# The first product of a graph convolution in seven block products, spread over four places of an LSTM pipeline

## The chip, the cores and the metric

The kernel runs on one core of a Trainium2 chip. The metric is the device time of one execution in microseconds (us). The core's engines run their own instruction queues side by side: TensorE (PE; its weight loads are listed as PEld), VectorE (DVE), ScalarE (ACT), GpSimd (POOL) and SyncE (SP), which here only starts transfers. All numbers are float32.

## The reference

Four layers work on x of 128 batches x 64 tokens x 256 channels. Each has the form x = x + f(relu(layernorm(x))). What matters here is layer 1, in which adj is the 64 x 64 adjacency matrix:

```python
h = relu(einsum('ts,bsh->bth', adj, x @ Wg0 + bg0))      # first graph convolution
h = relu(einsum('ts,bsh->bth', adj, h @ Wg1 + bg1))      # second graph convolution
for p in range(1, 5):                                    # four LSTMs, over windows of p tokens
    wins = h[:, :nw * p].reshape(B * nw, p, H)           # nw = T // p
    last = lstm_last(Wih[p-1], Whh[p-1], bih[p-1], bhh[p-1], wins)
    h = h.at[:, idx].set(last)                           # idx = p - 1, 2p - 1, ...
```

Each LSTM reads what the ones before it have written, so the four run one after another. Layer 0 is a network of two products with batch normalization, layers 2 and 3 are attention.

## The kernel before

The 8192 rows are cut into 16 chunks of 512 (index c), and the LSTM stage takes two chunks at a time: superchunk sc holds chunks 2sc and 2sc + 1, and runs the LSTMs for p = 1, 2, 3, 4 on them. The state lies with channels on the partitions, in two blocks of 128 (index k). A product of 256 x 256 weights with the state is made from seven products of 128 x 128 weight blocks, with sums and differences of blocks as operands: the function `differences` makes the four differences of the input blocks, and the sums of the weights are made once. In the LSTM steps the products of one gate add up in the PSUM banks x, y and z; between two products into a bank, ACT or DVE reads the partial sum.

While superchunk sc is in the LSTMs, the chunks of the next superchunk go through the two graph convolutions. `convolutions(c)` is a Python generator; what lies between two of its `yield`s is one unit. Its units in order: batch normalization (`scaled`), transposes, loads, the residual add (`add_squares`, L298), layer norm in four units, the product with adj (`aggregate`, L228), the copy from PSUM to SBUF (L1025), the product v with Wg0 (`product_v`, L934), its lower bound by a constant in place of bias and relu (`bounded`, L940), the product u with Wg1 (`product_u`, L948), its bias (`biased`, L954), and the second product with adj. In `product_u` the blocks of v are the weights that PE loads, and Wg1 is streamed.

The generator `lstms` yields too, and each of its yields has a number, its place. An ordinary yield goes on to the next whole number, a yield marked "a" to a half. The LSTM p=1 ends at place 3; p=2 has the places 4, 4.5, 5, 5.5, 6, 7; p=3 has 8 to 13; p=4 has 14, 14.5, 15 and so on to 21. Place 7 is after the last instruction of p=2, and place 13 after that of p=3. Lists say at which place each unit of a chunk is issued, the even chunk's list first:

```python
CONV = (3, 4, 5, 5.5, 7, 8, 9, 10, 10), (5, 5, 6, 9.5, 11, 11.5, 13, 14, 15, 15.5, 17, 18, 20)
BEGUN = (11, 11.5, 12, 14.5, 17, 17, 20, 21), (17.5, 19, 19.5, 21)
```

BEGUN holds the first units of the chunks after next, CONV the rest, FIRST stands for CONV in superchunk 0. The whole stage is under a manual schedule: each engine runs its instructions in the order in which the program issues them. Waits between engines are put in by the framework, from what an instruction reads and writes. At one place, the units of CONV come first, then those of the residual, of the next layer's work (`ahead`, lists AHEAD and LATE) and of BEGUN.

Before the change the even chunk has v at place 5, its bound at 5.5 and u at 7; the odd chunk has v at 13, its bound at 14 and u at 15. The DVE and ACT lines of the LSTM that are named further on: L1137 and L1192 copy a partial sum, L1140 and L1195 add one, L1101 is a gate's activation, L1158, L1165, L1265 and L1266 update the cell, L1159, L1166 and L1267 are its tanh, L1110, L1112 and L1116 write the new state, L327 to L330 are the four lines of `differences`. On GpSimd, L1252 multiplies two gates, and L99 and L100 belong to the layer norm.

PSUM has eight banks in this stage, of which the tag "ps" has two: they hold in turn the results of the products with adj, v and u. The SBUF tag "g" has three buffers, for transposed tiles of the residual and of the next layer. Chunks 0 and 1 go through `first_convolutions` in a start stage, where Wg0, Wg1 and LSTM weights are also loaded.

## Time and profile before

| | us |
|---|---|
| median of 3 runs (1841.59 to 1841.98) | 1841.59 |
| the profiled execution | 1841.82 |
| span of its records | 1839.9 |
| PE busy | 1813.3 (99%) |
| PE weight loads busy | 1531.8 (83%) |
| DVE busy | 1353.8 (74%) |
| ACT busy | 1061.4 (58%) |
| GpSimd busy | 656.8 (36%) |

The LSTM stage takes some 1210 us of the span, about 152 for each of the eight superchunks. The clock granted to PE was 0.999 of full speed. The profile lists two records for each matmul of 256 or 512 columns; [...]the time of a block is read from the chain or from the starts of its first and next instruction. In a line of the timeline the columns are: start in us, length in us, engine, line of the kernel, operation, what it writes and reads, its shape, how many instructions were merged, and, in brackets, the idle time of the engine before it and what ended that.

### The profile page before, as it was taken

The numbers are of one execution on the slowest core, as the hardware profiler recorded it, in microseconds if no ns is written. First come the engines' busy times: TensorE is split into PE (matmuls) and PEld (weight loads), VectorE is DVE, ScalarE is ACT, GpSimd is POOL, SyncE is SP. The second block draws the span as 40 slices with busy tenths as digits, with TensorE's granted clock in tenths as the row PEclk, the third lists the DMA queues.
The fourth block names the chain that finished last, engine by engine and source line by source line (L and its number), as shares of the span: only waits on it lengthen the run. The fifth ranks groups of instructions, "written<-read, shape, count | busy, mean of one in ns | idle before, by whom it ended". The sixth has DMA issues, their size and how long they took to land.

```text
span 1839.9 us, 41662 instructions
## 1 busy us (share of the span) xinstructions
PE 1813.3 (99%) x15847; PEld 1531.8 (83%) x15847; DVE 1353.8 (74%) x3475; ACT 1061.4 (58%) x2538; POOL 656.8 (36%) x916
## 2 busy tenths in 40 slices
PE   8999999999999999999999999999999999999998
PEld 6876866997897899699699789879968887898886
DVE  5768857577667777777777777776676677888897
ACT  5766636557457466655655746566565654455553
POOL 5865823223223321422321332232232215444542
PEclk9999999999999999999999999999999999999999
DMA  3213651233443342253443434225154146544534
GB/s 117 70 58 139 222 218 53 81 115 127 134 143 127 112 153 78 98 146 116 149 149 127 149 115 162 101 93 150 48 172 149 64 110 195 162 139 139 162 108 147
DMA packets 113415, 234.54 MB, mean 127 GB/s; under 512 B 11712, under 2 KB 77120, under 8 KB 113216
## 3 DMA queue, kind: packets, MB, share of 16 engines
q1 hardware_dynamic: 112320, 230.02, 38.5%
q8 instruction: 125, 2.05, 0.5%
q0 software_dynamic: 320, 1.05, 0.2%
q10 hardware_dynamic: 576, 0.82, 0.1%
q14 instruction: 74, 0.61, 0.1%
HBM read 164.21 MB, written 67.63 MB: 126 GB/s over the span
## 4 chain that ended last, share of the span: by engine, by line
PE 89%; DVE 5%; ACT 2%; POOL 2%; issue 1%; DMA 0%; SPq 0%; DVEq 0%; ACTq 0%; POOLq 0%
PE x L1186 23%; PE z L1186 11%; PE y L1186 6%; PE y L1133 4%; PE x L1368 4%; PE y L1368 3%; PE u L948 3%; PE v L934 3%; PE x L1133 3%; PE X L1938 3%; PE X L436 2%; PE X L512 2%; PE v L2062 2%; PE z L1133 2%; PE Y L1938 1%; PE X L1773 1%
## 5 line engine op out<-in xcount | busy, mean ns | idle before, releaser
L1101 ACT ACTIVATE l_gates<-l_gates,bias 128x256 f32<-128x256 f32 (+4 forms) x528 | 238.2, 498 | 210.9 <-DVE l_gates L1195 109.7
L1186 PE MATMUL x<-xd,wset 128*128 128x128 f32 (+2 forms) x1152 | 255.0, 303 | 0.8 <-ACT l_gates L1192 0.8
L1186 PE MATMUL x<-l_hd,wset 128*128 128x128 f32 (+2 forms) x1152 | 254.6, 303 | 0.0
L1252 POOL TENSOR_TENSOR l_gates<-l_gates 128x512 f32<-128x512 f32 (+2 forms) x48 | 75.3, 1570 | 368.0 <-ACT l_gates L1101 368.0
L1195 DVE TENSOR_TENSOR l_gates<-l_gates,x 128x128 f32<-128x128 f32 (+2 forms) x384 | 121.2, 321 | 97.8 <-PE x L1186 95.1
L1186 PEld LDWEIGHTS x<-xd,wset 128*128 128x128 f32 x1152 | 187.7, 191 | 6.4 <-issue 1.4
L1186 PEld LDWEIGHTS x<-l_hd,wset 128*128 128x128 f32 x1152 | 187.8, 191 | 5.0
L1195 DVE TENSOR_TENSOR l_gates<-l_gates,z 128x128 f32<-128x128 f32 (+2 forms) x384 | 102.3, 318 | 105.7 <-PE z L1186 103.7
L1186 PE MATMUL z<-l_hs,wset 128*128 128x128 f32 (+2 forms) x768 | 147.1, 304 | 0.7 <-DVE l_hs L1110 0.7
L1186 PE MATMUL z<-hT,wset 128*128 128x128 f32 (+2 forms) x768 | 146.2, 303 | 0.0
L1192 ACT COPY l_gates<-y 128x128 f32<-128x128 f32 (+2 forms) x192 | 53.2, 290 | 137.7 <-PE y L1186 131.5
L1186 PEld LDWEIGHTS z<-l_hs,wset 128*128 128x128 f32 x768 | 116.8, 191 | 5.8 <-DVE l_hs L1110 2.5
L1186 PEld LDWEIGHTS z<-hT,wset 128*128 128x128 f32 x768 | 117.1, 191 | 3.3
L1101 ACT ACTIVATE l_gates<-x,bias 128x128 f32<-128x128 f32 (+2 forms) x216 | 84.8, 393 | 28.6 <-PE x L1186 25.9
L327 POOL TENSOR_TENSOR xd<-hT 128x128 f32<-128x128 f32 (+2 forms) x72 | 43.2, 600 | 127.5 <-DVE hT L1112 113.8
L1186 PE MATMUL x<-hT,wset 128*128 128x128 f32 (+2 forms) x384 | 85.8, 305 | 0.0
L1186 PE MATMUL x<-l_hs,wset 128*128 128x128 f32 (+2 forms) x384 | 84.9, 303 | 0.0
L1186 PE MATMUL y<-l_hd,wset 128*128 128x128 f32 (+2 forms) x384 | 83.2, 309 | 0.0
L1267 ACT ACTIVATE l_gates<-l_cell 128x256 f32<-128x256 f32 (+2 forms) x144 | 55.3, 384 | 45.8 <-DVE l_cell L1266 45.3
L1186 PE MATMUL y<-xd,wset 128*128 128x128 f32 (+2 forms) x384 | 81.6, 304 | 0.0
L328 POOL TENSOR_TENSOR xd<-hT 128x128 f32<-128x128 f32 (+3 forms) x80 | 51.5, 644 | 67.0 <-DVE hT L1116 29.5
L1110 DVE TENSOR_TENSOR l_hs<-l_gates 128x256 f32<-128x256 f32 (+4 forms) x120 | 51.4, 428 | 29.6 <-ACT l_gates L1159 13.8
(408 smaller groups left out, 4696.8 us busy)
## 6 DMA issues: line engine op xcount, KB each, us to landing
wset<-wfar SPq DMA_DIRECT2D x96, 896.0 KB, 8.4
hT<-far_h SPq DMA_DIRECT2D x124, 128.0 KB, 4.7
far_h<-hm SPq DMA_DIRECT2D x16, 512.0 KB, 3.0
far_n<-xs SPq DMA_DIRECT2D x16, 512.0 KB, 3.4
xs<-far_n SPq DMA_DIRECT2D x64, 128.0 KB, 2.8
far_x<-xs SPq DMA_DIRECT2D x16, 512.0 KB, 3.9
x<-far_x SPq DMA_DIRECT2D x64, 128.0 KB, 3.9
xt<-in_x_dram SPq DMA_DIRECT2D x15, 512.0 KB, 3.9
```

The costliest lines, as they stand in the source:

```text
L328: lambda: ((third or engine).tensor_tensor(t3, b22, b12, OP.subtract), engine.tensor_tensor(t2, b22, t1, OP.subtract)),
L934: nc.tensor.matmul(banks[m], wg0_sb[:, k, m * P : (m + 1) * P], agg[:, k, :], start=(k == 0), stop=(k == KD - 1))
L948: nc.tensor.matmul(banks[j // 2][:, j % 2, :], v[:, k, j * P : (j + 1) * P], wg1_sb[:, k, :], start=(k == 0), stop=(k == KD - 1))
L1101: nc.scalar.activation(gate(q, c, part), src, AF.Tanh if q == 2 else AF.Sigmoid, bias=bs[:, q * KD + c : q * KD + c + 1])
L1133: nc.tensor.matmul(folded(self.psum(kind)), wsets[p, self.q][:, BLOCKS[kind][0], :], ox[0][kind], start=kind in (1, 5), stop=True, skip_gr ...
L1186: nc.tensor.matmul(folded(self.psum(kind)), wsets[p, self.q][:, BLOCKS[kind][i], :], (ox[self.s] if part == "x" else oh)[kind], start=firs ...
L1192: nc.scalar.copy(gate(self.q, kind // 5, halves[kind // 5]), self.psum(kind))
L1195: nc.vector.tensor_add(gate(self.q, *dst), gate(self.q, *a), self.psum(kind))
L1252: nc.gpsimd.tensor_mul(gates[:, 0, :, :n], gates[:, 0, :, :n], gates[:, 2, :, :n])
L1267: nc.scalar.activation(gate(2, c, part), cells[:, c, part], AF.Tanh)
L1368: nc.tensor.matmul(folded(ps(g, kind)), single_block(KINDS1[kind])[:, g, :], right[kind], start=kind in (2, 5, 1), stop=True, skip_group_c ...
L1938: nc.tensor.matmul(st[c, tag][:, i * CH // 2 : (i + 1) * CH // 2].rearrange("p (a n) -> p a n", n=P), w, operand3(c, kind), start=first an ...
```

## The change

Chunks 2 to 15 no longer make v by four products of 512 columns (two blocks of Wg0 for each half of the output). The new class `SevenV` makes it by seven products of 256 columns. After the copy from PSUM, GpSimd makes the four differences of the input's blocks in a tile of tag "g". The seven products go into two PSUM banks, the first called xx and zz by its halves, of the second only yy is used, in four units: products 2, 1 and 5 with ACT's copies of xx and yy into the input's own place; products 6 and 3 with one copy and one add; product 7 with two adds and two bounds; product 4 with the last bound, which reads PSUM. The last block of v comes to lie in the place of another one, so that `product_u` reads two blocks swapped; it takes the second half of the tokens first.

The lists get two entries more for each chunk: the even chunk has the four units at 5, 5.5, 6 and 7 and u at 7, the odd chunk at 13, 14, 14.5 and 15 and u at 15. Sums of the blocks of Wg0 are made once on GpSimd in the start stage. The bias bg1 is loaded into the tile c2 itself, and its own tile goes.

```diff
@@ start stage
-        bg1_sb = const.tile([P, D], F32, name="bg1_sb")
-        nc.sync.dma_start(bg1_sb, bg1.partition_broadcast(P))
+    nc.sync.dma_start(c2, bg1.partition_broadcast(P))
...
-                nc.vector.tensor_add(c2, c2_ps[:, :D], bg1_sb)
+                nc.vector.tensor_add(c2, c2, c2_ps[:, :D])
...
                 load_sets(6)
+                sums_of_wg0()
@@ product_u
-    def product_u(c, v):
+    def product_u(c, v, swapped=False):
+
         banks = [bank(f"u1_{c}_{t}").rearrange("p (j d) -> p j d", d=D) for t in range(NJ // 2)]
-        for j in range(NJ):
+        for j in (2, 3, 0, 1) if swapped else range(NJ):
             for k in range(KD):
-                nc.tensor.matmul(banks[j // 2][:, j % 2, :], v[:, k, j * P : (j + 1) * P],
+                at = (j + 2) % NJ if swapped and k else j
+                nc.tensor.matmul(banks[j // 2][:, j % 2, :], v[:, k, at * P : (at + 1) * P],
                                  wg1_sb[:, k, :], start=(k == 0), stop=(k == KD - 1))
         return banks
+
+    wg0_sums = w1.tile([P, 4, P], F32, name="wg0_sums")
+
+    def sums_of_wg0():
+        def a(k, m):
+            return wg0_sb[:, k, m * P : (m + 1) * P]
+
+        for d, u, v, op in ((0, a(0, 1), a(1, 1), OP.add), (1, wg0_sums[:, 0], a(0, 0), OP.subtract),
+                            (2, a(0, 0), a(0, 1), OP.subtract), (3, a(1, 0), wg0_sums[:, 1], OP.subtract)):
+            nc.gpsimd.tensor_tensor(wg0_sums[:, d], u, v, op)
+
+    class SevenV:
+
+        def __init__(self, c, y):
+            self.c, self.y = c, y
+            b = {(k, j): y[:, k, halves2[j]] for k in range(KD) for j in range(2)}
+            t = l1r.tile([P, 4, CH // 2], F32, tag="g", name=f"tv_{c}", bufs=3)
+            t = [t[:, i] for i in range(4)]
+            for f in differences(nc.gpsimd, t, b[0, 0], b[0, 1], b[1, 0], b[1, 1]):
+                f()
+            self.at = {1: b[0, 0], 2: b[1, 0], 3: b[1, 1], 4: t[3], 5: t[0], 6: t[1], 7: t[2]}
+            self.to = {(0, 0): b[0, 0], (0, 1): b[0, 1], (1, 0): b[1, 1], (1, 1): b[1, 0]}
+
+        def product(self, kind, ps, first=False):
+            if kind in (1, 2, 4):
+                m, k = {1: (0, 0), 2: (0, 1), 4: (1, 1)}[kind]
+                w = wg0_sb[:, k, m * P : (m + 1) * P]
+            else:
+                w = wg0_sums[:, {5: 0, 6: 1, 7: 2, 3: 3}[kind], :]
+            nc.tensor.matmul(ps, w, self.at[kind], start=first, stop=True, skip_group_check=True)
+
+        def add(self, part, ps):
+            nc.vector.tensor_add(self.to[part], self.to[part], ps)
+
+        def bound(self, m, dst, src):
+            dst, src = [a.rearrange("p (a n) -> p a n", n=P) for a in (dst, src)]
+            nc.vector.tensor_tensor(dst, src, nc1[:, m, None, :].to_broadcast([P, dst.shape[1], P]), OP.max)
+
+        def places(self):
+            xz, w = bank(f"vx_{self.c}"), bank(f"vy_{self.c}")
+            xx, zz, yy = xz[:, : CH // 2], xz[:, CH // 2 :], w[:, : CH // 2]
+            self.product(2, zz, True)
+            self.product(1, xx)
+            nc.scalar.copy(self.to[0, 0], xx)
+            self.product(5, yy, True)
+            nc.scalar.copy(self.to[1, 1], yy)
+            yield
+            self.product(6, xx)
+            nc.scalar.copy(self.to[0, 1], xx)
+            self.add((0, 0), zz)
+            self.product(3, yy)
+            yield
+            self.add((0, 1), yy)
+            self.product(7, xx)
+            self.add((1, 1), xx)
+            self.bound(0, self.y[:, 0], self.y[:, 0])
+            self.bound(1, self.to[1, 1], self.to[1, 1])
+            yield
+            self.product(4, xx)
+            self.bound(1, self.to[1, 0], xx)
+            yield
@@ convolutions, after the copy from PSUM
-        yield
-        banks = product_v(c, y)
-        yield
-        bounded(y, banks)
-        yield
-        banks = product_u(c, y)
+        v = SevenV(c, y)
+        yield
+        yield from v.places()
+        banks = product_u(c, y, swapped=True)
@@ the lists of places
-    CONV = (3, 4, 5, 5.5, 7, 8, 9, 10, 10), (5, 5, 6, 9.5, 11, 11.5, 13, 14, 15, 15.5, 17, 18, 20)
+    CONV = ((3, 4, 5, 5.5, 6, 7, 7, 8, 9, 10, 10),
+            (5, 5, 6, 9.5, 11, 11.5, 13, 14, 14.5, 15, 15, 15.5, 17, 18, 20))
-    FIRST = (0.5, 0.5, 1, 3, 3, 4, 4, 5, 5.5, 7, 8, 9, 10, 10), (2, 3, 4, 5, 5, 5.5, 6, 9.5, 11, 11.5, 13, 14, 15, 15.5, 17, 18, 20)
+    FIRST = ((0.5, 0.5, 1, 3, 3, 4, 4, 5, 5.5, 6, 7, 7, 8, 9, 10, 10),
+             (2, 3, 4, 5, 5, 5.5, 6, 9.5, 11, 11.5, 13, 14, 14.5, 15, 15, 15.5, 17, 18, 20))
```

## The prediction, made before the changed kernel was run

> **What bounds the kernel now.** I read the busy shares first, then the busy time by stage, then single instructions around the convolutions. The page's first part and the stretch of the third superchunk (us; busy time of PE, weight loads, DVE, ACT, POOL; clock; DMA share):
> ```profile
> PE 1813.3 (99%) x15847; PEld 1531.8 (83%) x15847; DVE 1353.8 (74%) x3475; ACT 1061.4 (58%) x2538; POOL 656.8 (36%) x916
> ...
> 580.00:732.00 152.00, 151.97 (x1145) 130.59 (x1144) 112.19 (x310) 91.16 (x238) 44.54 (x64) 1.00 0.37 122
> ```
> In the LSTM stage TensorE is idle 0.03 us of 152. So every column taken from it is gained, every wait put into it is lost, and nothing later makes up for a wait. The chain that ended last prices v and u:
> ```profile
> 609.90 3.43 PE v L934 x8
> 635.78 3.45 PE u L948 x16
> 680.76 3.43 PE v L934 x8
> 690.29 3.46 PE u L948 x16
> ```
> v is 4 products of 512 columns in 3.43 us, u 8 products of 256 columns in 3.45, so one 256-column product costs 0.431. Each block stands where the LSTM has a latency to hide. The timeline around u of convolution 6 (place 7, first line group) and 7 (place 15):
> ```profile
> 639.71 0.99 DVE L1116 TENSOR_TENSOR hT<-l_gates 128x256 f32<-128x256 f32 x2
> 640.62 1.28 DVE L954 TENSOR_TENSOR cv<-u,c 128x512 f32<-128x512 f32 x2
> ...
> 690.13 3.62 PE L948 MATMUL u<-wg_sb,cv 128*128 128x256 f32 x16
> 691.34 0.29 DVE L327 TENSOR_TENSOR l_hd<-l_hs 128x128 f32<-128x128 f32 x1
> 691.61 1.29 DVE L298 TENSOR_TENSOR xs<-xs,cv 128x512 f32<-128x512 f32 x2
> 692.82 0.42 DVE L1165 TENSOR_TENSOR l_cell<-l_gates 128x256 f32<-128x256 f32 x1
> 694.71 0.29 DVE L330 TENSOR_TENSOR l_hd<-l_hs,l_hd 128x128 f32<-128x128 f32 x1
> ```
> DVE still works on the LSTM's state while PE runs u: at place 7 until 640.70 (u ran 635.62 to 639.07), at place 15 until 695.00 (u ran 690.13 to 693.58). Today u needs nothing from that stretch, as v was bounded at 623.21 and 684.37.

> [...] The trace agrees (L1158 0.69, L1140 0.42), so the new SBUF-to-SBUF bounds get these prices. [...] the trace has GpSimd 256-column differences at 734 and at 929 ns (L330, L329)[...].

> **The change, part by part** (14 convolutions, one even and one odd in each superchunk 0 to 6).

> Removed and put in on PE: 3.43 us against 7 x 0.431 = 3.02, a gain of 0.41 each, 5.8 us in all, if nothing waits.

> GpSimd: four differences of some 0.74 = 3.0 us. Even: they follow the p=2 operands (end 605.39), so the third product of place 5 finds them; nothing follows until 613.84. Odd: after the copies at 673.77 they push the gate product L1252 from 675.18 to some 676.8, done at 678.4; its reader L1266 starts at 680.75. Both hidden; without that cover p=3's cell would be late by the excess. The scratch tile shares three "g" buffers, but at most two others are live when it comes: I take no wait.

> ACT: three copies of 0.37 each.

> Even convolution, numbers of the third superchunk. Place 5: v's block shrinks to three products, 1.29 us, so PE arrives 2.14 early. y<-l_hd must wait for L327 (ends 611.61), 0.2. z<-l_hs would come at 614.6 but needs the second L1110, which ends at 615.71, as four norm statistics stand ahead of its L1165 on DVE: 1.1. PE is 0.8 early; in superchunks 0 and 1, with no such statistics, 1.9 early. Place 5.5 adds two products (0.86), place 6 one (0.43): 0.4 late (0.7 early). At place 6 DVE now has two adds and two bounds, 0.42 + 0.42 + 0.69 + 0.42 = 1.95, ahead of the L1195 at 629.78. That add must read bank x before PE's next product into it: DVE is done at 632.1, PE is there at 631.7, so 0.4 is lost. PE and the chain behind it are **0.83 late** (first two: 0.23 early). Place 7: product 4, then its bound on DVE, then u. The bound is **queued behind L1116**. PE does product 4 and five products of u (2.6 us) and then stops, since the sixth takes as weights what that bound writes. L1116 ends 4.73 us after u's old start (5.08 in superchunk 2); then the bound 0.42, a restart of 0.29 (in the start stage L940 ended at 268.08, u began at 268.37), and the three products left, 1.29. Against u's old 3.45: 4.73 + 0.83 + 0.42 + 0.29 + 1.29 - 3.45 = 4.11 late (4.46 in superchunk 2; 3.05 in 0 and 1). Everything of p=3 is behind u on PE. Sum: 4 x 4.11 + 4.46 + 2 x 3.05 = 27.0.

> Odd convolution. Place 13: PE is again 2.14 early, and loses it: the first products of p=4 wait for L1112 (682.31), and product 6 waits for the copy of xx, which ACT reaches only after L1267 (684.09). With place 14's two products PE is level at 685.4 (before: 685.36). Place 14.5: the 1.95 us of DVE now stand ahead of L298 and L1165, which followed each other without a gap, so L1165, the second L1110 and L330 come 1.95 later. Place 15: the last bound is queued behind L330. L330 ended 4.87 after u's start: 4.87 + 1.95 + 0.42 + 0.29 + 1.29 - 3.45 = 5.37 late. In superchunk 6 there is no L298 and L1165 waited for ACT (1300.85, now 1302.2): 4.29 + 1.35 + 2.00 - 3.45 = 4.19. Sum: 6 x 5.37 + 4.19 = 36.4.

> Start stage: the four weight sums (some 0.5 each, as L1745) wait for wg_sb, issued at 240.17 with 2.9 to land; they end near 245.2, ahead of GpSimd's next work at 247.36, so nothing. bg1 now lands in c2: the same transfer, but one that may wait for c2's space with the loads of x behind it on SP (231.56, needed at 245.38). No row shows that; a c2 wait of up to 10 us is hidden, earlier space could gain a little. I take 0, with -1 to +4.

> Sum: 27.0 + 36.4 = 63.4. The profiled execution took 1841.82 with a span of 1839.9; it lies 0.23 above the median of 1841.59. So **1905.0**.

> **The rivals.**
> *Waits are covered, faster.* If the last bound were done when PE reaches the sixth product of u, only the gain of 5.8 would stay: 1836. That decides at 2.6 us after u's place: DVE must be through by then. For it: PE has early products to do. Against: DVE is busy with the LSTM until 4.73 and 4.87 after it. 4%.
> *The bound doesn't hold u up, but the rest stands.* If DVE took it ahead of the state's work, place 5 and 6 would cost some 1.3 in five even convolutions (0 in two), and the odd ones some 2.8, as product 4 needs the add that DVE reaches at 692.4: 26, so 1868. Against: L954 and L298 stand on DVE exactly where their places put them. 8%.
> *u waits as a whole.* If a wait went by tile or bank, the five early products would wait too: 2.16 x 14 = 30 more, 1935. Against: a product took l_hd at 310.07 while L328, issued ahead of it for another part of l_hd, began only at 310.93; so waits go by part. Banks: the first half of u can take the bank freed at place 6. 10%.
> *It doesn't do what it says.* The code gives 7 products of 256 columns for 4 of 512; the records will show it. No chance given.

> **How the numbers follow.** The forecast has 78%: 1892 to 1918, by +-0.5 us in each of the 14 sums and the start's bounds. 1866 to 1922 takes in the second rival and leaves out the first and third, with tails some 18%. A difference of 0.2% (3.7 us) is about what a measurement of this kernel can tell from no change. Faster: the first rival and a little, 0.05; within it 0.02; slower 0.93.

> **What would show it.** PE idle for some 10 us (the lateness and the 0.41 gained, twice) in each of superchunks 0 to 6, each of these 161 to 162 us long in place of 152, and superchunk 7 as before. The largest waits of PE are weight loads of u, put down to the last bound, 14 of them, of 2 to 3 us; next the odd convolutions' product 4, some 1.9, put down to the adds of place 14.5; small ones at z<-l_hs after L1110. Work grows without binding: DVE by 3 x 0.42 + 0.69 + 2 x 0.42 - 1.36 = 1.43 for each convolution, 20 us in all, ACT by 14 x 1.1 = 15, GpSimd by 14 x 3.0 + 2 = 44. The step at u is wrong if its eight products run without a gap, and the step at place 14.5 if L1165 isn't later there; the forecast is wrong if PE's idle time in these superchunks stays under 3 us each.

## The result, and the profile after

The changed kernel takes 1922.29 us (median of 4 runs, 1921.84 to 1922.54), the kernel before 1841.72 beside it: a ratio of 1.0436 (95% interval 1.0424 to 1.0448), 80.6 us slower. The forecast was 1905.0, so 63.4 slower; the direction held, and the stops of PE came where they were forecast; the size fell 17.3 us short, and the time lies 0.29 us beyond the upper end of the range.

First the page's busy times and its chain that ended last (before, PE had 89% of that chain and DVE 5%), then the stretch of the third superchunk by stage, with the columns as shown before:

```profile
PE 1840.4 (96%) x15931; PEld 1558.4 (81%) x15931; DVE 1371.5 (71%) x3531; ACT 1071.4 (56%) x2580; POOL 696.3 (36%) x976
...
PE 80%; DVE 11%; ACT 4%; POOL 2%; issue 2%; DMA 1%; DVEq 0%; SPq 0%; ACTq 0%; POOLq 0%
```
```profile
605.49:769.47 163.98, 156.22 (x1158) 135.03 (x1157) 114.47 (x317) 93.05 (x245) 49.94 (x72) 0.98 0.34 113
```

Two things stand in that line. PE now idles for 7.8 us of the superchunk where it idled for 0.03. And it is busy for longer, 156.2 us in place of 152.0, although seven products of 256 columns are less work than four of 512, while its clock has a mean of 0.98 in place of 1.00. The superchunks 0 to 6 became longer by 13.5, 12.2, 12.0, 11.6, 10.8, 12.4 and 8.0, in all 80.5; the start and superchunk 7 are as before.

What PE waited for most in the superchunks 0 to 6 (us in total, times, longest):

```profile
PE u L949 <- DVE cv L988: 32.2, 14, 2.8
PE vx L981 <- DVE cv L984: 11.3, 7, 1.6
PE z L1246 <- DVE l_hs L1170: 4.0, 5, 0.8
```

L988 is the bound in `SevenV`, L984 its add, L981 its product, L949 the product of u. The other lines have moved: L1110, L1112 and L1116 are now L1170, L1172 and L1176, L1165 is L1225, L1186 is L1246, L1133 is L1193, L954 is L1016. Each of the 14 u stops, for the bound, as forecast. The timeline at place 7 of the third superchunk, lines of PE and DVE:

```profile
662.31 1.89 PE L949 MATMUL u<-wg_sb,cv 128*128 128x256 f32 x8
...
665.62 0.99 DVE L1176 TENSOR_TENSOR hT<-l_gates 128x256 f32<-128x256 f32 x2
666.53 0.42 DVE L988 TENSOR_TENSOR cv<-vx,nc 128x256 f32<-128x256 f32 x1
667.00 3.78 PE L949 MATMUL u<-wg_sb,cv 128*128 128x256 f32 x8 [2.80 <-DVE cv L988]
670.58 1.33 PE L1193 MATMUL y<-hT,wset 128*128 128x168 f32 x4
```

The bound starts as L1176 ends, and u goes on as the bound ends. But u has done only four products by then (8 records), not five, and its second half takes 3.58 us to the next instruction, where four products take 1.72 at full clock (4 x 0.431). The profile by stages of a few us shows why (the eighth column, after POOL's busy time, is the clock that was granted):

```profile
667.00:670.50 3.50, 3.50 (x8) 2.86 (x9) 0.00 (x0) 0.00 (x0) 3.34 (x8) 0.50 1.02 349
670.50:674.00 3.50, 3.50 (x17) 3.42 (x16) 1.29 (x2) 1.76 (x6) 1.94 (x4) 0.63 0.50 90
674.00:680.00 6.00, 6.00 (x76) 5.47 (x78) 3.93 (x13) 1.98 (x6) 0.00 (x0) 1.00 0.00 1
```

From 666.24 to 673.07 PE has half the clock, with u's second half and the first products of p=3 in it. This happens after 9 of the 14 stops; the trace shows the halved clock for 34.1 us of these superchunks, ten times 3.41, and PE is busy in 33.0 of them. Half of that, 16.5 us, is my estimate of what the halved clock costs.

The same place in the odd convolution, where the clock stayed whole (1.00 in each stretch from 722 to 740), PE first and then DVE:

```profile
724.86 0.70 PE L981 MATMUL vx<-tv,wg_sb 128*128 128x256 f32 x2 [1.62 <-DVE cv L984]
725.47 1.99 PE L949 MATMUL u<-wg_sb,cv 128*128 128x256 f32 x8
729.44 1.99 PE L949 MATMUL u<-wg_sb,cv 128*128 128x256 f32 x8 [1.98 <-DVE cv L988]
```
```profile
724.06 0.41 DVE L984 TENSOR_TENSOR cv<-cv,vy 128x256 f32<-128x256 f32 x1
724.39 0.41 DVE L984 TENSOR_TENSOR cv<-cv,vx 128x256 f32<-128x256 f32 x1
724.73 1.02 DVE L988 TENSOR_TENSOR cv<-cv,nc 128x512 f32<-128x512 f32 x2
725.66 1.29 DVE L298 TENSOR_TENSOR xs<-xs,cv 128x512 f32<-128x512 f32 x2
726.87 0.42 DVE L1225 TENSOR_TENSOR l_cell<-l_gates 128x256 f32<-128x256 f32 x1
...
728.76 0.29 DVE L330 TENSOR_TENSOR l_hd<-l_hs,l_hd 128x128 f32<-128x128 f32 x1
728.97 0.42 DVE L988 TENSOR_TENSOR cv<-vx,nc 128x256 f32<-128x256 f32 x1
```

Two adds and two bounds stand ahead of L298 and L1225, and the last bound stands behind L330. Both are where the prediction put them.

### The profile page after: what moved, and what is told of

The parts are those of the page before. It is cut to its first block, busy times and chain, and to the rows that moved or that the text cites. A ratio compares the mean times of both kernels' runs of the same rounds, so it can differ in the third digit from the quotient of the medians.

```text
span 1920.0 us, 41959 instructions
## 1 busy us (share of the span) xinstructions
PE 1840.4 (96%) x15931; PEld 1558.4 (81%) x15931; DVE 1371.5 (71%) x3531; ACT 1071.4 (56%) x2580; POOL 696.3 (36%) x976
## 4 chain that ended last, share of the span: by engine, by line
PE 80%; DVE 11%; ACT 4%; POOL 2%; issue 2%; DMA 1%; DVEq 0%; SPq 0%; ACTq 0%; POOLq 0%
PE x L1246 20%; PE z L1246 10%; PE y L1246 5%; PE x L1428 4%; PE y L1193 3%; PE y L1428 3%; PE u L949 3%; PE X L2001 2%; PE X L436 2%; PE x L1193 2%; PE X L512 2%; PE v L2125 2%; PE z L1193 1%; PE Y L2001 1%; DVE l_gates L1200 1%
## 5 line engine op out<-in xcount | busy, mean ns | idle before, releaser
L1246 PE MATMUL x<-xd,wset 128*128 128x128 f32 (+2 forms) x1152 | 255.4, 303 | 2.2 <-DVE l_gates L1255 1.4
L1246 PE MATMUL x<-l_hd,wset 128*128 128x128 f32 (+2 forms) x1152 | 254.5, 303 | 0.0
L1246 PEld LDWEIGHTS x<-xd,wset 128*128 128x128 f32 x1152 | 187.1, 191 | 9.1 <-DVE l_gates L1255 2.7
L1246 PEld LDWEIGHTS x<-l_hd,wset 128*128 128x128 f32 x1152 | 187.8, 191 | 5.0
L1246 PE MATMUL z<-l_hs,wset 128*128 128x128 f32 (+2 forms) x768 | 147.6, 305 | 4.7 <-DVE l_hs L1170 4.7
L1246 PE MATMUL z<-hT,wset 128*128 128x128 f32 (+2 forms) x768 | 146.2, 303 | 0.0
L1252 ACT COPY l_gates<-y 128x128 f32<-128x128 f32 (+2 forms) x192 | 53.2, 290 | 164.6 <-PE y L1246 162.3
L1246 PEld LDWEIGHTS z<-l_hs,wset 128*128 128x128 f32 x768 | 116.3, 191 | 11.6 <-DVE l_hs L1170 8.5
L1246 PEld LDWEIGHTS z<-hT,wset 128*128 128x128 f32 x768 | 117.6, 191 | 3.7
L949 PE MATMUL u<-wg_sb,cv 128*128 128x256 f32 x224 | 68.2, 458 | 32.2 <-DVE cv L988 32.2
L327 POOL TENSOR_TENSOR xd<-hT 128x128 f32<-128x128 f32 (+2 forms) x72 | 42.2, 587 | 124.8 <-DVE hT L1172 111.0
L949 PEld LDWEIGHTS u<-wg_sb,cv 128*128 128x128 f32 x224 | 48.3, 223 | 47.6 <-DVE cv L988 40.0
L1246 PE MATMUL x<-hT,wset 128*128 128x128 f32 (+2 forms) x384 | 85.8, 305 | 0.0
L1246 PE MATMUL y<-l_hd,wset 128*128 128x128 f32 (+2 forms) x384 | 84.8, 313 | 0.3
L1246 PE MATMUL x<-l_hs,wset 128*128 128x128 f32 (+2 forms) x384 | 84.8, 303 | 0.0
L1246 PE MATMUL y<-xd,wset 128*128 128x128 f32 (+2 forms) x384 | 83.0, 309 | 0.0
```

The lines of the kernel that those rows point to most:

```text
L327: return [lambda: engine.tensor_tensor(t1, b12, b11, OP.subtract), lambda: ((third or engine).tensor_tensor(t3, b22, b12, OP.subtract), en ...
L949: nc.tensor.matmul(banks[j // 2][:, j % 2, :], v[:, k, at * P : (at + 1) * P], wg1_sb[:, k, :], start=(k == 0), stop=(k == KD - 1))
L1246: nc.tensor.matmul(folded(self.psum(kind)), wsets[p, self.q][:, BLOCKS[kind][i], :], (ox[self.s] if part == "x" else oh)[kind], start=firs ...
L1252: nc.scalar.copy(gate(self.q, kind // 5, halves[kind // 5]), self.psum(kind))
```

## The experiments

My theory after the result: the stops at u cost what the prediction says and two things more, a clock that falls to one half after many of them, and a bank that holds back the fifth product of u. The rival: the extra time is further waiting in the chain, from the added work of DVE, ACT and GpSimd. All times are medians, each compared with the kernel before on the same chip (1841.8 to 1842.4). I call a product or instruction idle when nobody reads its result, and PE's work cover where it fills the time in which the LSTM's chain isn't ready for PE's next product.

| kernel | us | ratio to before (95% interval) | against before, us |
|---|---|---|---|
| e1, last product and bound earlier | 1892.76 | 1.0274 (1.0257 to 1.0291) | +50.9 |
| e2, idle products ahead of u | 1907.77 | 1.0358 (1.0343 to 1.0374) | +65.9 |
| e3, even convolutions only | 1877.96 | 1.0199 (1.0184 to 1.0214) | +36.1 |
| e4, one product of eight left out | 1835.15 | 0.9964 (0.9951 to 0.9977) | -6.8 |
| e5a, even only, idle products | 1869.54 | 1.0152 (1.0137 to 1.0167) | +27.7 |
| e5b, e5a with another bank for u | 1866.74 | 1.0135 (1.0120 to 1.0150) | +24.9 |
| e6, e2 with the odd adds earlier | 1912.83 | 1.0386 (1.0371 to 1.0402) | +71.0 |
| e7, all of v earlier | 1873.44 | 1.0172 (1.0155 to 1.0189) | +31.6 |
| e8, before, v in two places | 1849.52 | 1.0041 (1.0027 to 1.0055) | +7.1 |
| e9, before, idle vector work | 1848.79 | 1.0034 (1.0021 to 1.0047) | +6.4 |
| e11, six even ones, earlier | 1857.08 | 1.0083 (1.0069 to 1.0097) | +15.0 |
| e10, e11 with the norm later | 1854.28 | 1.0067 (1.0054 to 1.0081) | +12.2 |

**e4: what the columns alone are worth.** In the kernel before, v of the chunks from 2 on is made of seven of its eight block products; the eighth is left out.

```diff
+        if c >= SUP:
+            for i in range(7):
+                m, k, h = i // 4, i % 2, halves2[i // 2 % 2]
+                nc.tensor.matmul(banks[m][:, h], wg0_sb[:, k, m * P : (m + 1) * P], agg[:, k, h],
+                                 start=(i % 4 == 0), stop=True, skip_group_check=True)
+            return banks
```

> The kernel before, whose v for chunks 2 to 15 is cut into 256-column products of which the last of eight is left out (its output lacks that term): PE's saving alone, with no waits, adds, copies or GpSimd work of the new scheme. If every column counts: 14 x 0.41 = 5.8 us faster, 1836. If the LSTM needs the whole of v's old block as cover: some waits come, and it stays above 1839.

6.8 us less (the interval is 4.2 to 9.0), where the prediction had 5.8. By the traces of the two kernels the superchunks 0 to 6 became 5.85 us shorter together, 0.42 for each of the 14 convolutions. So this is the most that the change could gain, and it needs all that it adds to be hidden.

**e1: the last bound half a place or a place earlier, u where it was.** Product 4 and its bound go from place 7 to 6, and from 15 to 14.5.

```diff
-    CONV = ((3, 4, 5, 5.5, 6, 7, 7, 8, 9, 10, 10),
-            (5, 5, 6, 9.5, 11, 11.5, 13, 14, 14.5, 15, 15, 15.5, 17, 18, 20))
+    CONV = ((3, 4, 5, 5.5, 6, 6, 7, 8, 9, 10, 10),
+            (5, 5, 6, 9.5, 11, 11.5, 13, 14, 14.5, 14.5, 15, 15.5, 17, 18, 20))
...
```

> Product 4 and the last bound go one place earlier (6 in place of 7, 14.5 in place of 15), so that the bound stands on DVE ahead of the end of the LSTM step. If the stop of u behind that bound is what costs most: u runs without a gap and without half clock. What is left is the wait of product 4 for the add ahead of it: even chunks 2.5 us late (0.6 in superchunks 0 and 1), odd chunks 3.8, as the z products stand behind the waiting product 4. 5 x 2.5 + 2 x 0.6 + 7 x 3.8 = 40: near 1882. If the extra work on DVE and ACT or the cut of v at the old places costs most, the time stays within 8 us of 1922.

29.5 us faster than the change: the place of the last bound is a large part of the loss. It is not the 40 expected. u no longer waits; product 4 does, since it now follows at once on the add that it takes:

```profile
PE vx L981 <- DVE cv L984: 25.7, 14, 2.5
```

The clock falls here too, with stops of up to 2.5 us: its mean is 0.993 in the profiled run, and in the LSTM stage the trace of e1 still has five stretches at half clock, 23.9 us in all (three of 3.41 us and two of 6.83). The gain at u was partly turned into another wait.

**e2: PE kept at work through part of the stop.** Sixteen transposes of a constant tile, whose result nobody reads, are put ahead of each u.

```diff
+        for i in range(16 if swapped else 0):
+            nc.tensor.transpose(banks[1][:, 0, :P], ident, ident)
         for j in (2, 3, 0, 1) if swapped else range(NJ):
```

> 16 idle transposes (some 1.8 us of PE work, not part of the computation's result) stand ahead of each of the 14 u blocks, so that PE is idle 1.8 us less at the stop. If the halved clock after the stop is the missing term: no u block runs at half clock, the mean clock is back at 0.999, and the time falls by 8 to 14 us, to 1908 to 1914, although PE does 25 us more work. If the clock plays no part and the rest of u is slow for another reason: 1922, or more where the transposes outlast the stop.

More work for PE, and 14.5 us less time. The granted clock of the profiled run is 1.000 in place of 0.991, and no halved stretch is left in the LSTM stage. The bound comes when it came; what PE waits for it has become short, and u's halves run at full speed. The odd convolution of the third superchunk:

```profile
714.46 0.70 PE L983 MATMUL vx<-tv,wg_sb 128*128 128x256 f32 x2 [1.62 <-DVE cv L986]
714.99 1.91 PE L947 MATMUL u<-ident 128*128 128x128 f32 x16
716.74 1.89 PE L951 MATMUL u<-wg_sb,cv 128*128 128x256 f32 x8
719.02 1.99 PE L951 MATMUL u<-wg_sb,cv 128*128 128x256 f32 x8 [0.39 <-DVE cv L990]
```

The filler takes nothing away from the added work of DVE, ACT or GpSimd, so the rival can't explain the 14.5 us. That the clock costs about that much is shown; the estimate from the halved stretches was 16.5.

**e3 and e5a: even convolutions alone, without and with the idle products.** The odd ones are as before.

```diff
-        v = SevenV(c, y)
-        yield
-        yield from v.places()
-        banks = product_u(c, y, swapped=True)
+        if c % SUP == 0:
+            v = SevenV(c, y)
+            yield
+            yield from v.places()
+            banks = product_u(c, y, swapped=True)
+        else:
+            yield
+            banks = product_v(c, y)
+            yield
+            bounded(y, banks)
+            yield
+            banks = product_u(c, y)
...
```

> Only the even chunks make v in seven products, the odd ones have the old way and the old places. If the costs of the two kinds simply add up as forecast: even 27.0, with 7 x 0.43 for the fifth early product of u that waits too and some 7 for the halved clock 37: near 1878. If the odd chunks alone carry the loss: under 1855; if the even ones do: over 1900.

> Only the even convolutions in seven products, and 16 idle transposes on TensorE ahead of each u. It is the base for the next kernel. Clock theory: the same even convolutions without the filler took 1878.0 with five half-clock windows of 3.41 us; the filler took 14.5 us off the changed kernel, which had ten such windows in its LSTM stage, so here some 7 to 8 us: 1870, and no half-clock window. If the even convolutions alone owe nothing to the clock: 1878 or more.

In both, the odd list is that of the kernel before. Both came within 0.5 us of what was expected. They split the loss. At full clock (0.999 in the profiled run of e5a, 1.000 in that of e2) the seven even convolutions cost 27.7 us (e5a against before) and the seven odd ones 38.2 (e2 against e5a). With the 14.5 us of the clock the sum is the whole loss again, but that is no test, since each part is the difference of two of the same runs. A test is e3 against e5a: without the idle products e3 takes 8.4 us longer, and in the five halved stretches of e3 PE is busy for 16.2 us, half of which is 8.1.

**e5b: the bank.** The half of the tokens that u takes last goes to a bank of tag z, where the change has it wait for the bank that product 4 wrote and the last bound reads.

```diff
-        banks = [bank(f"u1_{c}_{t}").rearrange("p (j d) -> p j d", d=D) for t in range(NJ // 2)]
+        banks = [bank(f"u1_{c}_{t}", "z" if swapped and not t else "ps").rearrange("p (j d) -> p j d", d=D)
+                 for t in range(NJ // 2)]
```

> As the kernel before it in this call, but u's second half of tokens goes to a bank of the LSTM's tag z, not to the one that product 4 used, so that only the data of the last bound hold it, no longer the bank. Theory (u stops after four products because of the bank, 0.43 each): the fifth product of u runs ahead of the stop, which is 0.43 shorter seven times: 3 us less, 1867. Rival (the bank costs nothing, the data alone stop u): the stop stays after four products and the time as it was, within 1 us. A little may be lost again where the LSTM's own z product now waits for the add after u.

2.8 us less than e5a, 0.40 for each of the seven convolutions. The timeline of u in the third superchunk's even convolution, e5a first, then e5b:

```profile
645.91 1.89 PE L951 MATMUL u<-wg_sb,cv 128*128 128x256 f32 x8
648.85 1.99 PE L951 MATMUL u<-wg_sb,cv 128*128 128x256 f32 x8 [1.04 <-DVE cv L990]
```
```profile
644.76 2.32 PE L952 MATMUL u<-wg_sb,cv 128*128 128x256 f32 x10
647.70 1.56 PE L952 MATMUL u<-wg_sb,cv 128*128 128x256 f32 x6 [0.62 <-DVE cv L991]
```

Now ten records, five products, come ahead of the stop, and the stop is 0.42 shorter. So the bank held back the fifth product in the change, and data alone the sixth.

**e6: the odd adds out of the way of L298.** On e2, the odd list has 12, 13, 14, 15 for the four units of v.

> The changed kernel with the filler (1907.8), and in the odd convolutions the four places 13, 14, 14.5, 15 moved to 12, 13, 14, 15: the 1.95 us of VectorE that stood ahead of the state's work at 14.5 now stand at 14, and product 4 comes 0.5 place after the adds that it takes. Theory (the block of 1.95 us ahead of L298 and L1225 at 14.5 is 1.95 of each odd convolution's lateness): 1.95 x 7 = 14 us less, 1894. Rival (that block only displaces other waiting): within 3 us of 1908.

A miss: 5.1 us slower than e2, where 14 less were expected. The wait of product 4 shrank from 9.7 us to 2.9 in the superchunks 1 to 6, but others took its place: 5.6 for GpSimd's operands of p=4 (y<-xd, none in e2), 4.5 in place of 2.6 for L1172, 12.8 in place of 8.2 for u. So in that junction, the end of p=3 and the start of p=4, moving DVE's work from 14.5 to 14 frees nothing. e6 also leaves PE one product less at place 13, two in place of three, and no run parts this loss of cover from DVE's work at place 14.

**e7: all of v ahead, so that the last bound is done when PE reaches u.** Without idle products. In the even convolutions the first product with adj (the aggregate) and its copy move ahead too, to 0 and 1.

```diff
-    CONV = ((3, 4, 5, 5.5, 6, 7, 7, 8, 9, 10, 10),
-            (5, 5, 6, 9.5, 11, 11.5, 13, 14, 14.5, 15, 15, 15.5, 17, 18, 20))
+    CONV = ((0, 1, 3, 4, 5, 5.5, 7, 8, 9, 10, 10),
+            (5.5, 5.5, 6, 9.5, 11, 11.5, 12, 13, 14, 14.5, 15, 15.5, 17, 18, 20))
...
```

> The changed kernel without filler; all of v is moved ahead so that its last bound is queued on VectorE one place or more before u: in even convolutions (from superchunk 1) the aggregate at 0, its copy at 1, products at 3, 4, 5, 5.5 and u at 7 as before; in odd ones 12, 13, 14, 14.5 and u at 15. In superchunk 0 the even ones only have product 4 at 6. Theory (the lateness is what VectorE still has to do when PE reaches u, and the half clock follows from it): u no longer stops in superchunks 1 to 6, nearly all of the 80 goes: 1841, within 8 either way, since the 5.8 of fewer columns is paid back where smaller pieces cover less of what PE waits for. Rival (the time went into the added work of VectorE, ScalarE and GpSimd wherever it stands): over 1880.

Half right. u doesn't wait at all, its 16 records run in one piece (first line), and 49.0 of the 80.6 us are gone. But 31.6 stay, which the theory did not have. The lines on which PE waits in the third superchunk, after that the even convolution's first, then the odd one's:

```profile
646.33 3.62 PE L949 MATMUL u<-wg_sb,cv 128*128 128x256 f32 x16
```
```profile
621.97 0.67 PE L1246 MATMUL y<-xd,wset 128*128 128x256 f32 x2 [0.60 <-ACT l_gates L1161]
626.80 1.99 PE L1246 MATMUL z<-l_hs,wset 128*128 128x256 f32 x8 [0.81 <-DVE l_hs L1170]
...
694.14 0.71 PE L1193 MATMUL y<-hT,wset 128*128 128x128 f32 x4 [0.75 <-DVE hT L1172]
...
696.63 0.70 PE L981 MATMUL vx<-tv,wg_sums 128*128 128x256 f32 x2 [0.49 <-DVE cv L984]
...
699.61 0.68 PE L1193 MATMUL y<-xd,wset 128*128 128x128 f32 x4 [0.94 <-POOL xd L329]
```

From the superchunk's first product to the even convolution's second aggregate it takes 68.86 us (before: 646.80 - 579.63 = 67.17), from there to the odd one's 62.68 (before: 59.83). So an even convolution costs 1.69 and an odd one 2.85, and seven of both 31.8. These are the places 5 and 13, where v stood in one piece of 3.43 us, and where 0.43 and 0.86 us of it now stand.

**e8 and e9: cover and vector work, each by itself, in the kernel before.** e8 makes v of the same four products of 512 columns, the first half at 4.5 and 12, the second at 5 and 13. e9 leaves v whole and puts three idle DVE instructions of 256 columns ahead of its bound.

```diff
@@ e8
...
-        banks = product_v(c, y)
+        banks = product_v(c, y, half=0)
+        yield
+        product_v(c, y, banks, half=1)
...
@@ e9
         yield
+        for i in range(3):
+            half = y[:, 0, : CH // 2]
+            nc.vector.tensor_tensor(half, half, half, OP.max)
         bounded(y, banks)
```

> The kernel before, v still in four products of 512 columns and no other work, but its first half (1.73 us) half a place or a place earlier (4.5 and 12) and only its second half at 5 and 13. Theory (what is left of 31.6 us when u no longer stops is lost cover: at 5 and 13 PE waits for the LSTM's chain, and v's 3.45 us in one piece filled that time): the odd ones lose 1.73 each, since the changed kernel's trace shows no slack there, 12 in all; the even ones some 0.5 each, 3.5 in all: 1857, at most 1866 if the even ones have no slack either. Rival (the rest is the added work of VectorE, ScalarE and GpSimd in the chain): within 3 us of 1841.8.

> The kernel before, with three idle VectorE instructions of 128x256 (some 0.3 to 0.4 us each) ahead of v's bound at places 5.5 and 14; v and u on TensorE as they were. Theory of lost cover: VectorE has room where v and u stand in one piece each, within 5 us of 1841.8. Rival (the added vector work is on the chain wherever it stands): 1.0 to 1.26 for each of the 14 convolutions, 1856 to 1860.

Neither theory has it alone: 7.1 us, where lost cover was to cost some 15 and the rival nothing, and 6.4, where lost cover had nothing and the rival 14 to 18. Measured as for e7, the even convolution loses nothing in either (67.17 and 67.03 to the second aggregate, before 67.17), the odd one 1.08 and 0.91 (60.91 and 60.74, before 59.83). PE's line of e9 at that place, and the wait of PE's weight loads in e8:

```profile
690.17 0.68 PE L1136 MATMUL y<-xd,wset 128*128 128x128 f32 x4 [0.77 <-POOL xd L329]
```
```profile
PEld y L1135 <- DVE hT L1114: 4.9, 7, 0.7
```

(L1114 is L1112 before, L1135 and L1136 are L1133.) At the junction of p=3 and p=4 there is little room: 1.73 us less of cover cost 1.1, and 1.64 us more of DVE's work (686.90 to 688.54) cost 0.9. At place 5 there is room for each of the two. The seven products take away more cover there, and add work too. That lost cover and added work together make up the 31.6 us of e7 is argued from these two runs, which cost 7.1 and 6.4; no run adds the two alone to the kernel before, and none tells what the earlier aggregate costs.

**e11 and e10: the best version that I could find.** Seven products in the even convolutions of superchunks 2 to 7 only, at 3, 5, 5.5 and 6, with the aggregate and its copy at 0 and 1 as in e7; e10 also moves the next layer's norm statistics (four records of 2.14 us in all with their aggregates) out of the chain at place 4.5.

```diff
-    CONV = ((3, 4, 5, 5.5, 6, 7, 7, 8, 9, 10, 10),
+    CONV = ((0, 1, 3, 5, 5.5, 6, 7, 8, 9, 10, 10),
...
@@ e10
-    LATE = (4.5, 4.5, 5.5, 9, 19.5), (9.5, 9.5, 11, 12, 21)
+    LATE = (5.5, 5.5, 7, 9, 19.5), (9.5, 9.5, 11, 12, 21)
```

> Seven products only in the even convolutions of superchunks 2 to 7 (six of the fourteen), all others in four: aggregate at 0, its copy at 1, products at 3, 5, 5.5 and 6, u at 7 as before. Where all convolutions were moved ahead, the trace shows the even one 1.69 late by its second aggregate, of which 0.60 for the copies at place 5 and 0.81 for l_hs behind 2.14 us of norm statistics on VectorE. With 0.43 more cover at 5: some 1.2 late each, 7 in all, 1849. If the seven products owe those waits to something else than this place: within 2 us of 1842.

> The kernel before it in this call, and the 2.14 us of norm statistics moved from place 4.5 to 5.5, where VectorE was idle for 2.6 us, their use from 5.5 to 7. It is the version that could beat both: theory (the even junction has room once the statistics are out of the chain): no wait is left and each of the six keeps 0.41, 2.5 us: 1839.4, which is less than these runs may tell from no change. Rival (smaller pieces cover too little whatever VectorE does): 0.5 to 1 late each, 1845 to 1848.

Both missed: 15.0 and 12.2 us slower than before, where 7 slower and 2.5 faster were expected. In e10 that is 2.0 for each of the six, on average. What PE waits for in e11 and then in e10, from superchunk 1 on:

```profile
PE z L1254 <- DVE l_hs L1178: 4.7, 6, 0.8
PE y L1201 <- ACT l_gates L1205: 3.6, 5, 0.8
PE x L1254 <- DVE l_gates L1263: 2.9, 6, 0.5
```
```profile
PE y L1201 <- ACT l_gates L1205: 4.4, 10, 0.8
PE x L1254 <- DVE l_gates L1263: 2.8, 6, 0.7
...
PE z L1254 <- DVE l_hs L1178: 0.7, 1, 0.7
```

Moving the statistics removed the wait that it was meant for (4.7 to 0.7), and 2.8 us of time. The other two stay: an add of the LSTM that now comes behind those of v (L1263 is L1195 before), and the copy of a partial sum at the start of an LSTM (L1205, before L1137). None of these versions beat the kernel before.

## Why the prediction was right or wrong

- **What bounds.** Right. PE had no idle time to give, and each wait at u came out as lost time. The chain at place 7, L1176 and then the bound and then u, and the one at place 15 behind L330 came as written, and so did u's stop within its own products: neither the covered wait, nor a wait for u as a whole, nor a bound ahead of the state's work.
- **The small terms.** z<-l_hs waits 0.81 (its weight load 1.2), forecast 1.1. Product 4 of the odd convolution waits 1.62, forecast some 1.9. The gain was 0.42 for each convolution in the trace of e4, forecast 0.41. DVE grew by 17.7 us, ACT by 10 and GpSimd by 39.5, forecast 20, 15 and 44. In the third superchunk PE idles for 7.8 us, forecast some 10; part of the loss came as slow work instead of idle time. Superchunk 7 and the start stage are unchanged, as forecast.
- **The sums at full clock.** 27.0 and 36.4 were forecast, 27.7 and 38.2 measured (e5a; e2 less e5a, which includes what the idle products cost): 65.9 against 63.4.
- **The failed step is what follows the stop, "a restart of 0.29, and the three products left, 1.29".** It lets PE go on at full speed, so a slower clock after the wait was put at nothing. After 9 of the 14 stops PE went on at half speed, eight times for 3.41 us and once for 6.83. That cost 14.5 us by e2, out of the 17.3 that the forecast fell short. The restart itself, taken from one row of the start stage, was not too small: where the clock stayed whole, u went on 0.05 us after the bound's end (729.39 to 729.44) and its four products took 1.83 us (831.33 to 833.16, in the last section), 1.88 together, where the prediction's prices for four give 0.29 + 1.72 = 2.01. The superchunks 1 to 6, forecast at 161 to 162 us, take 160.2 to 164.6.
- **A second step failed, "PE does product 4 and five products of u".** It does four, since u's second bank is the one that the last bound reads. By e5b that is 0.40 each in the even convolutions; if the odd ones lost as much, 5.6 for 14. The prediction had asked of the banks only where the first half of u goes. As the whole at full clock is only 2.5 above the forecast, the other terms together came out some 3 lower: part of the miss was cancelled by luck. Some 2 of these 3 lie in the even convolutions, which cost 24.9 without the halved clock and the bank (e5b), forecast 27.0. Two terms were too large in the trace: the restart, by 0.13, and the two adds and two bounds, summed up to 1.95, which take 1.60 from the first one's start to the next instruction (724.06 to 725.66), as each record starts before the one ahead of it has ended. No run takes these terms one by one.
- **The range.** Its upper end was made of +-0.5 us for each sum. No case in it had PE slower after a wait. The trace of before could not show what a wait of 2 to 3 us does in a stage where PE had none, so this cost was unknown, and the upper end left no room for it.

## What to carry to other kernels

Where an engine is busy for all of a stage, price a new wait as the wait and what comes after it: here TensorE's clock fell to one half after 9 of the 13 stops of 1.97 to 2.80 us at u, and with idle matmuls in the stops the kernel was 14.5 us faster than with the bare stops. Before a product is cut into smaller ones that need other engines between them, ask what the whole one covered: v in one piece hid a latency of the LSTM twice in each superchunk, and 0.42 us of saved columns can't pay for the 1.7 and 2.9 us that a convolution loses even where u no longer stops (e7). When the place of a wait is known, look at both things that a stopped product needs, its operands and its bank.

## What the runs showed of the hardware that I had not expected

The clock fell after stops that the prediction had priced as waits only. Stops of 1.97 to 2.80 us were enough (0.50 of full clock after the one that ended at 667.00), and the length of a stop doesn't decide. The same stop of 2.80 us in the next superchunk left the clock whole:

```profile
826.64 1.89 PE L949 MATMUL u<-wg_sb,cv 128*128 128x256 f32 x8
831.33 1.99 PE L949 MATMUL u<-wg_sb,cv 128*128 128x256 f32 x8 [2.80 <-DVE cv L988]
833.16 0.73 PE L1193 MATMUL y<-hT,wset 128*128 128x168 f32 x4
```

while a stop of 1.98 us that began at 889.17 in that superchunk was followed by a second half of u of 3.45 us. All stretches at half clock in the LSTM stage last 3.41 us or twice that.

The traces show more. The nine halved stretches begin whole multiples of 3.413 us apart: 338.56, 400.00 and 502.40 are 18 and 30 such lengths apart, and so on up to 1219.20. So the whole stage can be cut into windows of that length from any of them. The stop of 2.80 us at 664.20 lies mostly in one window, the one at 828.53 is split between two (after the window its length, then PE's busy time; the clock is again the eighth column):

```profile
662.83:666.24 3.41, 1.37 (x7) 0.87 (x5) 2.82 (x7) 2.65 (x7) 0.59 (x1) 1.00 1.11 235
826.67:830.08 3.41, 1.86 (x9) 1.30 (x7) 2.65 (x7) 2.54 (x7) 0.58 (x1) 1.00 1.09 253
830.08:833.49 3.41, 2.16 (x11) 1.96 (x12) 1.17 (x4) 0.40 (x2) 2.40 (x5) 1.00 1.00 362
```
